# First cross attention of a perceiver block: the softmax's probabilities turned by VectorE and DMA in place of TensorE

## The chip, the cores and the metric

The kernel runs as one program on one NeuronCore of a Trainium2 chip. The metric is the time on the device in microseconds (us); of several executions the median is taken. One further execution was recorded by the hardware profiler. All durations of single instructions come from that one.

The engines are TensorE (PE; its weight loads are shown apart as PEld), VectorE (DVE), ScalarE (ACT), GpSimd (POOL) and SyncE (SP, which here only issues DMAs).

## The reference, cut to what matters

A block of six residual layers works on `x` (32 batches of 64 tokens, 256 features) beside a context `ctx` (32 batches of 256 rows, 256 features). All is float32. The change is in the first layer, a cross attention whose keys and values are the context's rows and the tokens themselves:

```python
def _L0_xattn_ref(image_embeds, latents, ..., Wq, Wkv, Wo):   # ctx, layernorm(x)
    x = layer_norm(image_embeds, ln1_g, ln1_b)      # 32 x 256 x 256
    l = layer_norm(latents, ln2_g, ln2_b)           # 32 x 64 x 256
    q = l @ Wq                                      # 16 heads of 64
    kv_in = jnp.concatenate([x, l], axis=1)         # 320 keys
    k, v = jnp.split(kv_in @ Wkv, 2, axis=-1)
    w = jnp.einsum('bhqd,bhkd->bhqk', q * scale, k * scale)
    w = jax.nn.softmax(w, axis=-1)
    out = jnp.einsum('bhqk,bhkd->bhqd', w, v)
    return out.transpose(0, 2, 1, 3).reshape(B, S_lat, INNER) @ Wo
```

The other layers are a linear attention, a gated feed-forward, a second cross attention, a recurrent gate layer and a mixture of eight experts.

## The kernel before, in words

**An order planned on the host.** Nearly every instruction is first recorded with a length in us, a `rank` (when it should come) and the buffers that it needs, in an object `pl` (class `Plan`). `Plan.run` (line 299) then plays all five engines against these lengths and emits the instructions one after the other: of those that can start first, the one of lowest rank. The order of each engine is thus fixed before the kernel runs, from the model's lengths (`PlanEngine.length`, line 474) and not from what happens on the chip. Copies out of PSUM may go to ACT or to DVE (`pl.copy`, `pl.either`), whichever the model finds earlier. A DMA costs its issuing engine 0.06 us in this model. Because one helper line emits everything, the profile gives line L375 for nearly all instructions; they are told apart by their tiles.

**Buffers.** One large SBUF tile, the arena, holds everything but small vectors; each kind of tile (`ar.put`, from line 649) has one or more fixed places, taken in turn. PSUM is eight banks of 512 floats per partition, all of one kind (`bank`).

**The first layer** goes through 32 batches b, two to a 128-row tile of tokens (16 tiles), four to a group (8 groups), in these steps:

- `l0_context` (777): loads two batches of context into `cx` (2 places) and normalises them.
- `l0_queries` (805), once in four batches: normalises the tokens (`la`, and `ls`, its two halves swapped by two DMAs), multiplies by Wq (PSUM `pq`) and then, head by head, by Wk (PSUM `pqk`), so that scores can be taken directly against the context. The result is one tile `qk` for the group, with one place: 16 heads stand in 8 pairs j, a pair's two heads and 64 tokens being 128 columns.
- `l0_keys` (857): transposes the batch's context into `cT` and puts the tokens' columns beside it, once on each side: 64 + 256 + 64 columns.
- `l0_scores` (872): for each of the 8 pairs, two passes over 128 features give `sc`, 128 rows (2 heads x 64 tokens) by 320 keys, in one PSUM bank. DVE takes the negated maximum (`nmax`), ACT takes the exponential with its sum (`sm`) into `pr`, DVE inverts `sm` and multiplies the 320 columns by it: one small and one larger DVE instruction for each pair. The pairs come as jj = 0 (j = 0, 2, 4, 6) and jj = 1; the keys' order is tokens-context for jj = 0 and context-tokens for jj = 1, so that in `pr` the two token parts stand side by side.
- `l0_applied` (902): the probabilities must stand with the keys on the partitions. Per batch TensorE transposes 16 blocks of 128 x 128 (`pTp`, four to a bank) and 4 more for the token keys (`plp`); five copies bring them to SBUF (`pT00` to `pT11`, `pl`). Then `pu` = context^T times probabilities: per half of the features and per jj two matmuls of 512 columns over 128 keys, and one over the 64 token keys; for these last the two jj use the upper and the lower half of the array's rows. Copies go to `uT`.
- `l0_projected` (939), once in two batches: `uT` times Wv (PSUM `po`), times Wo (`pw`), added to `x`.

A float32 matmul appears as two MATMUL instructions, a transpose as one. The model's lengths for PE are written beside the code, e.g. `with pl.together(T4)` with T4 = 0.46 us for four transposes.

What sets the order around the change is the ranks: scores of batch b have b - 0.7 to b, `l0_applied` has b, the projection 2t + 1.6. `pl.run(12.0)` lets the plan look 12 ranks ahead, so that the second stage's first work fills in at the end of this layer. Later tiles of the second stage take over places of the arena when the first layer's last tiles leave them.

Of the kernel before, what the change touches and what calls it, by code (L numbers as in the profile page):

```python
# [438 lines left out]
class PlanEngine:  # L439
# [33 lines left out]
    @staticmethod  # L473
    def length(engine, name, args, kw):

        if "dma" in name:
            return 0.06 if "indirect" not in name else 1.55 if "compute_op" in kw else 1.25
# [21 lines left out]
def kernel(ctx: ExitStack, tc: tile.TileContext, d: dict, out: bass.AP):  # L499
# [96 lines left out]
    def experts_constants():  # L596
# [10 lines left out]
        nc.gpsimd.memset(rst[:, :, 0:1], 0.0)  # L607
        c["ones"] = ones = e1.tile([P, P], F32, tag="ones", name="ones")
        nc.gpsimd.memset(ones, 1.0)

# [15 lines left out]
    ec = experts_constants()  # L626
    irow, slot, sp1, i8, rk, rst, ones, tok0, before, thr = (
        ec[n] for n in ("irow", "slot", "sp1", "i8", "rk", "rst", "ones", "tok0", "before", "thr")
    )
# [3 lines left out]
    with ExitStack() as sa:  # L633
        ARENA = 44928
        arena = sa.enter_context(tc.tile_pool(name="arena", bufs=1)).tile([P, ARENA], F32, tag="arena", name="arena")
# [19 lines left out]
        ar.put(1, "cx", 1024, 14336, 15360)  # L655
        ar.put(1, "cT", 768, 16384, 17152)
        ar.put(0, "gbcol", 256, 17920, 18176)
        ar.put(1, "qk", 8192, 17920)
        ar.put(1, "uT", 4096, 26112)
        ar.put(1, "pr", 640, *range(30208, 35328, 640))  # L660
        for n, tag in enumerate(("pT00", "pT01", "pT10", "pT11", "pl")):
            ar.put(1, tag, 512, 35328 + 1024 * n, 35840 + 1024 * n)
        ar.put(1, "oT", 1024, 40448)

        for tag, size, *at in (
# [15 lines left out]
            ("g_tmp", 128, 41472), ("g_tmp2", 128, 41600), ("g_h", 128, 41728),  # L681
            ("a_wq", 512, 41856), ("a_wkv", 1024, 42368), ("rows_a", 1024, 43392),
        ):
# [121 lines left out]
        def l0_queries(g):  # L805
# [37 lines left out]
            pl.rank = G * g - 0.9  # L843
            qk = ar.tile([P, KD, G, 8, 2, S], F32, tag="qk", name=f"qk{g}")
            for n in range(8):
                j = 2 * (n % 4) + n // 4
                pqk = [bank([P, KD, G * S], f"pqk{g}_{j}_{i}") for i in range(2)]
                with pl.together(1.0):
                    for kd in range(KD):
                        for i in range(2):  # L850
                            h_ = slice(64 * i, 64 * i + 64)
                            mm(pqk[i][:, kd], wkT[h_, j, kd * P : (kd + 1) * P], q[h_, j, :], start=True, stop=True)
                for i in range(2):
                    pl.copy(qk[:, :, :, j, i, :], pqk[i].rearrange("p k (b s) -> p k b s", b=G))
            return la, ls, lt, qk

        def l0_keys(b, lt, cx):

            pl.rank, pl.lane = b - 1.2, "k"
            b2, b4 = b % 2, b % G  # L860
            cT = ar.tile([P, KD, SK + S], F32, tag="cT", name=f"cT{b}")
# [5 lines left out]
            for c0 in (0, SK):  # L867
                pl.gpsimd.tensor_copy(cT[:, :, c0 : c0 + S], lt[:, :, b4 * S : (b4 + 1) * S])
            pl.copy(cT[:, :, S:SK], pst)
            return cT  # L870

        def l0_scores(b, cT, qk):

            pl.lane = "s"
            prs = [ar.tile([P, 2 * SK], F32, tag="pr", name=f"pr{b}_{i}", bufs=8) for i in range(4)]
            for jj in range(2):
                k0 = 0 if jj else S
                for jp in range(4):  # L880
                    j = 2 * jp + jj
                    pl.rank = b - 0.7 + 0.1 * (4 * jj + jp)
                    sc = bank([P, SK], f"sc{b}_{j}")
                    with pl.together(1.1):
                        for kd in range(KD):
                            mm(
                                sc,
                                qk[:, kd, b % G, j].rearrange("p i s -> p (i s)"),
                                cT[:, kd, k0 : k0 + SK],
                                start=(kd == 0),  # L890
                                stop=(kd == KD - 1),
                            )
                    nmax = sp.tile([P, 1], F32, tag="nmax", name=f"nmax{b}_{j}")
                    pl.vector.tensor_reduce(nmax, sc, AX.X, ALU.max, negate=True)
                    sm = sp.tile([P, 1], F32, tag="sm", name=f"sm{b}_{j}")
                    pr = prs[jp][:, jj * SK : (jj + 1) * SK]
                    pl.scalar.activation(pr, sc, AF.Exp, bias=nmax, accum_out=sm)
                    pl.vector.reciprocal(sm, sm)
                    pl.vector.tensor_scalar(pr, pr, sm, None, ALU.mult)
            return prs  # L900

        def l0_applied(b, prs, cx, la, ls, uT):

            pl.rank, pl.lane = float(b), "a"
            bp, b2 = b // 2 % 2, b % 2
            pT = [[], []]
            for jj in range(2):
                for n in range(2):
                    pT_ = ar.tile([P, 4, P], F32, tag=f"pT{jj}{n}", name=f"pT{b}_{jj}_{n}")
                    pTp = bank([P, 4, P], f"pTp{b}_{jj}_{n}")  # L910
                    with pl.together(T4):
                        for jp in range(4):
                            c0 = jj * SK + n * P + (S if jj else 0)
                            tr(pTp[:, jp, :], prs[jp][:, c0 : c0 + P], ident)
                    pl.copy(pT_, pTp)
                    pT[jj].append(pT_)
            pl_ = ar.tile([P, 4, P], F32, tag="pl", name=f"pl{b}")
            pl_ps = bank([P, 4, P], f"plp{b}")
            with pl.together(T4):
                for jp in range(4):  # L920
                    tr(pl_ps[:, jp, :], prs[jp][:, S2 : S2 + P], ident)
            pl.copy(pl_, pl_ps)

            lk = [la, ls] if b2 == 0 else [ls, la]
            for kd in range(KD):
                f_ = slice(kd * P, (kd + 1) * P)
                pus = [bank([P, 4, P], f"pu{b}_{kd}_{jj}") for jj in range(2)]
                for jj in range(2):
                    with pl.together(1.75):
                        for n in range(2):  # L930
                            mm(pus[jj], cx[:, 2 * b2 + n, f_], pT[jj][n], start=(n == 0), stop=False)
                with pl.together(0.9):
                    for jj in range(2):
                        h_ = slice(64 * jj, 64 * jj + 64)
                        mm(pus[jj], lk[jj][h_, bp, f_], pl_[h_], start=False, stop=True)
                for jj in range(2):
                    pl.copy(uT[:, kd, 4 * jj : 4 * jj + 4, :, b2, :], pus[jj].rearrange("p j (i s) -> p j i s", i=2))

# [26 lines left out]
        for t in range(NTILE):  # L965
            cx = l0_context(t)
            uT = None
            for b in (2 * t, 2 * t + 1):
                if b % G == 0:
                    la, ls, lt, qk = l0_queries(b // G)  # L970
                cT = l0_keys(b, lt, cx)
                prs = l0_scores(b, cT, qk)
                if uT is None:

                    uT = ar.tile([P, KD, 8, 2, 2, S], F32, tag="uT", name=f"uT{t}")
                l0_applied(b, prs, cx, la, ls, uT)
            l0_projected(t, uT)
# [541 lines left out]
        def cells(part, gate, cap, first=None):  # L1519
# [15 lines left out]
            pl.scalar.copy(gT, gT_ps)  # L1535
            v.tensor_tensor_scan(rank, ones, sel, 0.0, ALU.mult, ALU.add)
            cnt = rank[:, P - 1 : P]
# [277 lines left out]
        v.tensor_reduce(ext, thr_, AX.X, ALU.add)  # L1815
        v.tensor_tensor_scan(cum, ones[:, 0:E], ext, 0.0, ALU.mult, ALU.add)
        v.tensor_tensor(ext, cum, ext, ALU.subtract)
# [105 lines left out]
```

## Time and profile before

| | us |
|---|---|
| median of 3 runs | 1720.64 |
| lowest, highest | 1719.38, 1720.93 |
| the profiled execution's own time | 1723.92 |
| its span, first to last instruction | 1722.2 |
| TensorE busy | 1653.6 (96%) |
| VectorE busy | 1034.1 (60%) |
| ScalarE busy | 696.6 (40%) |
| GpSimd busy | 316.1 (18%) |
| mean granted TensorE clock | 0.988 |

The first score matmul starts at 31.2 us and the last first-layer projection ends near 920 us: the first layer is a little over half of the span. In a busy share the ends of matmuls are modelled, and two matmuls can overlap; how fast PE goes is read from the distance between the starts of successive matmuls. The group rows give a mean duration of one instruction, which for a matmul is longer than that distance. A releaser behind an arrow is what ended an engine's idle time.

### The profile page before, as it was taken

What the parts mean: (1) busy time and instruction counts of PE and PEld (TensorE: products, weight loads), DVE (VectorE), ACT (ScalarE), POOL (GpSimd) and SP (SyncE); (2) the same over time, 40 slices, a digit from 0 to 9 for tenths busy, and PEclk for the clock granted to TensorE, in tenths of its full rate; (3) what the DMA queues carried; (4) which work ended last, traced back from release to release, by engine and by line L of the source; (5) the groups of instructions that cost most, each with busy time, mean ns of one, the idle gap of its engine ahead of it and who ended that gap; (6) DMA issues with size and microseconds to landing.
All of it is one profiled execution on the core that took longest, in us unless ns stands there. A gap on an engine that the chain in (4) does not pass through costs nothing. (4 is left out here: it accounts for less than half of the span.)

```text
span 1722.2 us, 26712 instructions
## 1 busy us (share of the span) xinstructions
PE 1653.6 (96%) x9866; PEld 1174.4 (68%) x9866; DVE 1034.1 (60%) x3430; ACT 696.6 (40%) x1830; POOL 316.1 (18%) x413
## 2 busy tenths in 40 slices
PE   7999999999999999999998799999999998999996
PEld 6666666766666766666565576777777776788885
DVE  7546464555554644645444578878888787853131
ACT  4334343443433433434331145545455455623232
POOL 5102120121111210211001211212202121133233
PEclk9999999999999999999999899999999999999998
DMA  6000000000000000001001000000100112255292
GB/s 206 13 7 25 7 25 13 6 20 13 19 7 13 13 13 6 19 7 59 25 1 59 13 1 26 26 19 20 38 13 26 58 44 73 68 162 166 38 295 57
DMA packets 50548, 74.09 MB, mean 43 GB/s; under 512 B 5231, under 2 KB 40880, under 8 KB 50416
## 3 DMA queue, kind: packets, MB, share of 16 engines
q1 hardware_dynamic: 44896, 64.42, 11.9%
q0 software_dynamic: 5520, 7.94, 2.2%
q8 instruction: 79, 1.29, 0.3%
q14 instruction: 53, 0.43, 0.1%
HBM read 63.63 MB, written 7.47 MB: 41 GB/s over the span
## 5 line engine op out<-in xcount | busy, mean ns | idle before, releaser
L375 PE MATMUL pu<-arena 128*128 128x512 f32 (+1 forms) x768 | 299.1, 613 | 0.0
L375 PE MATMUL sc<-arena 128*128 128x320 f32 x1024 | 298.6, 437 | 0.0
L375 PEld LDWEIGHTS sc<-arena 128*128 128x128 f32 x1024 | 187.5, 190 | 88.2 <-issue 21.1
L375 PEld LDWEIGHTS pu<-arena 128*128 128x128 f32 (+1 forms) x768 | 111.4, 188 | 164.6 <-issue 164.4
L375 ACT ACTIVATE arena<-sc,nmax 128x320 f32<-128x320 f32 x256 | 135.4, 529 | 182.3 <-DVE nmax L375 182.2
L375 POOL TENSOR_TENSOR arena<-arena 128x256 f32<-128x256 f32 (+3 forms) x104 | 137.5, 1325 | 255.1 <-DVE arena L375 214.9
L375 DVE TENSOR_REDUCE nmax<-sc 128x1 f32<-128x320 f32 x256 | 124.3, 489 | 90.6 <-PE sc L375 84.7
L375 DVE COPY arena<-pu 128x512 f32<-128x512 f32 x64 | 44.3, 692 | 215.6 <-PE pu L375 215.4
L375 ACT ACTIVATE arena<-arena,xnm 128x256 f32<-128x256 f32 x256 | 127.2, 499 | 58.6 <-DVE xnm L375 58.0
L375 ACT COPY arena<-pu 128x512 f32<-128x512 f32 x64 | 37.5, 586 | 242.9 <-PE pu L375 242.9
L375 DVE TENSOR_SCALAR arena<-arena,sm 128x320 f32<-128x320 f32 x256 | 117.5, 459 | 9.0
L375 DVE CUSTOM_DVE_ANT_0 arena<-xsc,arena 128x256 f32<-128x256 f32 x256 | 100.9, 420 | 9.3 <-ACT arena L375 3.8
L375 POOL TENSOR_TENSOR r_c<-ve_c,mhalf 128x4 f32<-128x4 f32 x16 | 16.3, 1019 | 310.0 <-DVE sm L375 258.7
L375 PEld LDWEIGHTS pTp<-ident,arena 128*128 128x128 f32 x512 | 59.4, 141 | 14.3 <-ACT arena L375 2.3
L375 PE MATMUL pTp<-ident,arena 128*128 128x128 f32 x512 | 67.6, 274 | 0.9 <-DVE arena L375 0.8
L375 PE MATMUL xpTp<-ident,arena 128*128 128x128 f32 x512 | 63.7, 274 | 2.2 <-ACT arena L375 1.8
L375 PE MATMUL xav<-arena 128*128 128x256 f32 x256 | 63.0, 391 | 0.4 <-DVE arena L375 0.4
L375 PEld LDWEIGHTS xpTp<-ident,arena 128*128 128x128 f32 x512 | 57.3, 141 | 8.8 <-DVE arena L375 2.9
L375 PE MATMUL xak<-arena 128*128 128x512 f32 x128 | 62.9, 617 | 0.1
L375 PE MATMUL mepha<-arena 128*128 128x256 f32 x256 | 60.0, 385 | 1.4 <-ACT arena L375 1.4
L375 PE MATMUL pq<-arena 128*128 128x256 f32 x256 | 60.1, 380 | 0.7 <-ACT arena L375 0.7
L375 ACT COPY arena<-xpTp 128x512 f32<-128x512 f32 x80 | 44.5, 585 | 39.0 <-PE xpTp L375 39.0
(407 smaller groups left out, 2916.3 us busy)
## 6 DMA issues: line engine op xcount, KB each, us to landing
arena<-in_m_w SPq DMA_DIRECT2D x26, 1024.0 KB
arena<-in_ctx SPq DMA_DIRECT2D x32, 256.0 KB
arena<-in_ctxT SPq DMA_DIRECT2D x16, 512.0 KB
x<-in_x SPq DMA_DIRECT2D x16, 128.0 KB
arena<-in_l0x_wkv SPq DMA_DIRECT2D x2, 1024.0 KB
arena<-arena SPq DMA_DIRECT2D x16, 128.0 KB
out<-x SPq DMA_DIRECT2D x16, 128.0 KB
xd<-arena SPq DMA_DIRECT2D x16, 128.0 KB
```

The costliest lines, as they stand in the source:

```text
L375: r = getattr(real, name)(*[get(a) for a in args], **{k: get(a) for k, a in kw.items()})
```

## The change

In the first layer:

- The 20 TensorE transposes per batch, their five PSUM banks and their five copies go. In their place DVE transposes 32 x 32 blocks: for each jj, two instructions of 512 columns and one of 256 write from `pr` into a new tile `bT` (one place), in which each group of 32 partitions still holds the wrong rows of blocks. Then 16 DMAs per batch, issued by SP, move blocks between the four groups of partitions into `pT` (2 places): DMA (k, a) takes partitions 32a to 32a+31, column group k, five runs of 128 floats per partition, to partitions 32k to 32k+31. That is 160 runs of 512 bytes, 80 KB; 16 of them are 1.25 MB per batch.
- `pr` now holds one jj of a batch (four pairs by 320 columns, 3 places). The normalisation is done for four pairs at once: one reciprocal of 4 values and one tensor_tensor multiply of 1280 columns with a broadcast operand, in place of four reciprocals and four tensor_scalar multiplies of 320.
- The keys' order is context-tokens for all pairs, so `cT` loses its third part and GpSimd one of its two copies.
- `pu`'s matmuls read `pT` through a pattern of runs of 32 columns, where they read 512 consecutive columns. Their number is the same.
- `qk` is eight tiles, one for each pair, with eight places, where it was one tile; the scores take them pair by pair.
- Ranks: scores at b - 1.6 + ..., the normalisation and transposes 0.3 below the last score of their jj. The model's cost of issuing a plain DMA goes from 0.06 to 0.4 us for all DMAs of the kernel; its length for the pair of token-key matmuls goes from 0.9 to 1.04.

In the mixture layer the constant tile of ones is dropped: two cumulative sums are written with add and max in place of multiply and add, with the same sizes. The places in the arena are laid out anew; it grows by 128 columns.

```diff
         if "dma" in name:
-            return 0.06 if "indirect" not in name else ...
+            return 0.4 if "indirect" not in name else ...
...
-        ar.put(1, "cT", 768, 16384, 17152)
+        ar.put(1, "cT", 640, 16384, 17024)
-        ar.put(1, "qk", 8192, 17920)
+        ar.put(1, "qk", 1024, *range(17664, 25856, 1024))
-        ar.put(1, "pr", 640, *range(30208, 35328, 640))
-        for n, tag in enumerate(("pT00", "pT01", "pT10", "pT11", "pl")):
-            ar.put(1, tag, 512, 35328 + 1024 * n, 35840 + 1024 * n)
+        ar.put(1, "pr", 1280, 29952, 31232, 32512)
+        ar.put(1, "bT", 2560, 33792)
+        ar.put(1, "pT", 2560, 36352, 38912)
...
         def l0_scores(b, cT, qk):
             pl.lane = "s"
-            prs = [ar.tile([P, 2 * SK], F32, tag="pr", ...) for i in range(4)]
+            B_ = 32
+            bT = ar.tile([P, 5, 4, 4, B_], F32, tag="bT", name=f"bT{b}")
             for jj in range(2):
-                k0 = 0 if jj else S
+                pr = ar.tile([P, 4, SK], F32, tag="pr", name=f"pr{b}_{jj}")
+                sm = sp.tile([P, 4], F32, tag="sm", name=f"sm{b}_{jj}")
                 for jp in range(4):
                     j = 2 * jp + jj
-                    pl.rank = b - 0.7 + 0.1 * (4 * jj + jp)
+                    pl.rank = b - 1.6 + 0.1 * (4 * jj + jp)
...
-                    pl.scalar.activation(pr, sc, AF.Exp, bias=nmax, accum_out=sm)
-                    pl.vector.reciprocal(sm, sm)
-                    pl.vector.tensor_scalar(pr, pr, sm, None, ALU.mult)
-            return prs
+                    pl.scalar.activation(pr[:, jp, :], sc, AF.Exp, bias=nmax, accum_out=sm[:, jp : jp + 1])
+                pl.rank -= 0.3
+                pl.vector.reciprocal(sm, sm)
+                pl.vector.tensor_tensor(pr, pr, sm.unsqueeze(2).to_broadcast([P, 4, SK]), ALU.mult)
+                for n in range(2):
+                    pl.vector.transpose(
+                        bT[:, 2 * n + jj].rearrange("p k j c -> p j k c"),
+                        pr[:, :, n * P : (n + 1) * P].rearrange("p j (k c) -> p j k c", c=B_),
+                    )
+                pl.vector.transpose(
+                    bT[:, 4, 2 * jj : 2 * jj + 2].rearrange("p k j c -> p j k c"),
+                    pr[:, :, S2:SK].rearrange("p j (k c) -> p j k c", c=B_),
+                )
+            pT = ar.tile([P, 5, 4, 4, B_], F32, tag="pT", name=f"pT{b}")
+            for k in range(4):
+                for a in range(4):
+                    pl.sync.dma_start(
+                        out=pT[B_ * k : B_ * k + B_, :, a].rearrange("p m j c -> p m (j c)"),
+                        in_=bT[B_ * a : B_ * a + B_, :, k].rearrange("p m j c -> p m (j c)"),
+                    )
+            return pT
...
         def l0_applied(b, pT, cx, la, ls, uT):
-            pT = [[], []]
-            for jj in range(2):
-                for n in range(2):
-                    pT_ = ar.tile([P, 4, P], F32, tag=f"pT{jj}{n}", name=f"pT{b}_{jj}_{n}")
-                    pTp = bank([P, 4, P], f"pTp{b}_{jj}_{n}")
-                    with pl.together(T4):
-                        for jp in range(4):
-                            c0 = jj * SK + n * P + (S if jj else 0)
-                            tr(pTp[:, jp, :], prs[jp][:, c0 : c0 + P], ident)
-                    pl.copy(pT_, pTp)
-                    pT[jj].append(pT_)
-            pl_ = ar.tile([P, 4, P], F32, tag="pl", name=f"pl{b}")
-            pl_ps = bank([P, 4, P], f"plp{b}")
-            with pl.together(T4):
-                for jp in range(4):
-                    tr(pl_ps[:, jp, :], prs[jp][:, S2 : S2 + P], ident)
-            pl.copy(pl_, pl_ps)
...
-                            mm(pus[jj], cx[:, 2 * b2 + n, f_], pT[jj][n], start=(n == 0), stop=False)
-                with pl.together(0.9):
+                            rhs = pT[:, 2 * n + jj].rearrange("p a j c -> p j a c")
+                            mm(pus[jj], cx[:, 2 * b2 + n, f_], rhs, start=(n == 0), stop=False)
+                with pl.together(1.04):
...
-            v.tensor_tensor_scan(rank, ones, sel, 0.0, ALU.mult, ALU.add)
+            v.tensor_tensor_scan(rank, sel, sel, 0.0, ALU.add, ALU.max)
```

More of the change, by code (lines that the diff above doesn't have):

```diff
@@ L476, in length @@
         if "dma" in name:
-            return 0.06 if "indirect" not in name else 1.55 if "compute_op" in kw else 1.25
+            return 0.4 if "indirect" not in name else 1.55 if "compute_op" in kw else 1.25
         o = args[0] if args else kw["out"]
@@ L607, in experts_constants @@
         nc.gpsimd.memset(rst[:, :, 0:1], 0.0)
-        c["ones"] = ones = e1.tile([P, P], F32, tag="ones", name="ones")
-        nc.gpsimd.memset(ones, 1.0)
         c["tok0"] = tok0 = e1.tile([P, 1], F32, tag="tok0", name="tok0")
@@ L626 @@
     ec = experts_constants()
-    irow, slot, sp1, i8, rk, rst, ones, tok0, before, thr = (
-        ec[n] for n in ("irow", "slot", "sp1", "i8", "rk", "rst", "ones", "tok0", "before", "thr")
+    irow, slot, sp1, i8, rk, rst, tok0, before, thr = (
+        ec[n] for n in ("irow", "slot", "sp1", "i8", "rk", "rst", "tok0", "before", "thr")
     )
@@ L633 @@
     with ExitStack() as sa:
-        ARENA = 44928
+        ARENA = 45056
         arena = sa.enter_context(tc.tile_pool(name="arena", bufs=1)).tile([P, ARENA], F32, tag="arena", name="arena")
@@ L655 @@
         ar.put(1, "cx", 1024, 14336, 15360)
-        ar.put(1, "cT", 768, 16384, 17152)
-        ar.put(0, "gbcol", 256, 17920, 18176)
-        ar.put(1, "qk", 8192, 17920)
-        ar.put(1, "uT", 4096, 26112)
-        ar.put(1, "pr", 640, *range(30208, 35328, 640))
-        for n, tag in enumerate(("pT00", "pT01", "pT10", "pT11", "pl")):
-            ar.put(1, tag, 512, 35328 + 1024 * n, 35840 + 1024 * n)
-        ar.put(1, "oT", 1024, 40448)
+        ar.put(1, "cT", 640, 16384, 17024)
+        ar.put(0, "gbcol", 256, 17664, 17920)
+        ar.put(1, "qk", 1024, *range(17664, 25856, 1024))
+        ar.put(1, "uT", 4096, 25856)
+        ar.put(1, "pr", 1280, 29952, 31232, 32512)
+        ar.put(1, "bT", 2560, 33792)
+        ar.put(1, "pT", 2560, 36352, 38912)
+        ar.put(1, "oT", 1024, 41472)
         for tag, size, *at in (
@@ L681 @@
             ("g_tmp", 128, 41472), ("g_tmp2", 128, 41600), ("g_h", 128, 41728),
-            ("a_wq", 512, 41856), ("a_wkv", 1024, 42368), ("rows_a", 1024, 43392),
+            ("a_wq", 512, 42496), ("a_wkv", 1024, 43008), ("rows_a", 1024, 44032),
         ):
@@ L843, in l0_queries @@
             pl.rank = G * g - 0.9
-            qk = ar.tile([P, KD, G, 8, 2, S], F32, tag="qk", name=f"qk{g}")
+            qk = [None] * 8
             for n in range(8):
                 j = 2 * (n % 4) + n // 4
+                qk[j] = ar.tile([P, KD, G, 2, S], F32, tag="qk", name=f"qk{g}_{j}")
                 pqk = [bank([P, KD, G * S], f"pqk{g}_{j}_{i}") for i in range(2)]
@@ L853, in l0_queries @@
                 for i in range(2):
-                    pl.copy(qk[:, :, :, j, i, :], pqk[i].rearrange("p k (b s) -> p k b s", b=G))
+                    pl.copy(qk[j][:, :, :, i, :], pqk[i].rearrange("p k (b s) -> p k b s", b=G))
             return la, ls, lt, qk
@@ L860, in l0_keys @@
             b2, b4 = b % 2, b % G
-            cT = ar.tile([P, KD, SK + S], F32, tag="cT", name=f"cT{b}")
+            cT = ar.tile([P, KD, SK], F32, tag="cT", name=f"cT{b}")
             pst = bank([P, KD, S2], f"tr_c{b}")
@@ L866, in l0_keys @@
                         tr(pst[:, kd, i * P : (i + 1) * P], cx[:, 2 * b2 + i, kd * P : (kd + 1) * P], ident)
-            for c0 in (0, SK):
-                pl.gpsimd.tensor_copy(cT[:, :, c0 : c0 + S], lt[:, :, b4 * S : (b4 + 1) * S])
-            pl.copy(cT[:, :, S:SK], pst)
+            pl.gpsimd.tensor_copy(cT[:, :, S2:SK], lt[:, :, b4 * S : (b4 + 1) * S])
+            pl.copy(cT[:, :, 0:S2], pst)
             return cT
@@ L876, in l0_scores @@
             pl.lane = "s"
-            prs = [ar.tile([P, 2 * SK], F32, tag="pr", name=f"pr{b}_{i}", bufs=8) for i in range(4)]
+            B_ = 32
+            bT = ar.tile([P, 5, 4, 4, B_], F32, tag="bT", name=f"bT{b}")
             for jj in range(2):
-                k0 = 0 if jj else S
+                pr = ar.tile([P, 4, SK], F32, tag="pr", name=f"pr{b}_{jj}")
+                sm = sp.tile([P, 4], F32, tag="sm", name=f"sm{b}_{jj}")
                 for jp in range(4):
                     j = 2 * jp + jj
-                    pl.rank = b - 0.7 + 0.1 * (4 * jj + jp)
+                    pl.rank = b - 1.6 + 0.1 * (4 * jj + jp)
                     sc = bank([P, SK], f"sc{b}_{j}")
@@ L887, in l0_scores @@
                                 sc,
-                                qk[:, kd, b % G, j].rearrange("p i s -> p (i s)"),
-                                cT[:, kd, k0 : k0 + SK],
+                                qk[j][:, kd, b % G].rearrange("p i s -> p (i s)"),
+                                cT[:, kd, :],
                                 start=(kd == 0),
@@ L894, in l0_scores @@
                     pl.vector.tensor_reduce(nmax, sc, AX.X, ALU.max, negate=True)
-                    sm = sp.tile([P, 1], F32, tag="sm", name=f"sm{b}_{j}")
-                    pr = prs[jp][:, jj * SK : (jj + 1) * SK]
-                    pl.scalar.activation(pr, sc, AF.Exp, bias=nmax, accum_out=sm)
-                    pl.vector.reciprocal(sm, sm)
-                    pl.vector.tensor_scalar(pr, pr, sm, None, ALU.mult)
-            return prs
-        def l0_applied(b, prs, cx, la, ls, uT):
+                    pl.scalar.activation(pr[:, jp, :], sc, AF.Exp, bias=nmax, accum_out=sm[:, jp : jp + 1])
@@ L904, in l0_applied @@
+            pT = ar.tile([P, 5, 4, 4, B_], F32, tag="pT", name=f"pT{b}")
[6 more added lines that the diff above has]
+            return pT
+        def l0_applied(b, pT, cx, la, ls, uT):
             pl.rank, pl.lane = float(b), "a"
@@ L926, in l0_applied @@
                 f_ = slice(kd * P, (kd + 1) * P)
-                pus = [bank([P, 4, P], f"pu{b}_{kd}_{jj}") for jj in range(2)]
+                pus = [bank([P, 4, 4, 32], f"pu{b}_{kd}_{jj}") for jj in range(2)]
                 for jj in range(2):
@@ L930, in l0_applied @@
                         for n in range(2):
-                            mm(pus[jj], cx[:, 2 * b2 + n, f_], pT[jj][n], start=(n == 0), stop=False)
-                with pl.together(0.9):
+                            rhs = pT[:, 2 * n + jj].rearrange("p a j c -> p j a c")
+                            mm(pus[jj], cx[:, 2 * b2 + n, f_], rhs, start=(n == 0), stop=False)
+                with pl.together(1.04):
                     for jj in range(2):
                         h_ = slice(64 * jj, 64 * jj + 64)
-                        mm(pus[jj], lk[jj][h_, bp, f_], pl_[h_], start=False, stop=True)
+                        rhs = pT[h_, 4].rearrange("p a j c -> p j a c")
+                        mm(pus[jj], lk[jj][h_, bp, f_], rhs, start=False, stop=True)
                 for jj in range(2):
-                    pl.copy(uT[:, kd, 4 * jj : 4 * jj + 4, :, b2, :], pus[jj].rearrange("p j (i s) -> p j i s", i=2))
+                    pl.copy(
+                        uT[:, kd, 4 * jj : 4 * jj + 4, :, b2, :],
+                        pus[jj].rearrange("p j (i a) c -> p j i (a c)", i=2),
+                    )
         def l0_projected(t, uT):
@@ L971 @@
                 cT = l0_keys(b, lt, cx)
-                prs = l0_scores(b, cT, qk)
+                pT = l0_scores(b, cT, qk)
                 if uT is None:
                     uT = ar.tile([P, KD, 8, 2, 2, S], F32, tag="uT", name=f"uT{t}")
-                l0_applied(b, prs, cx, la, ls, uT)
+                l0_applied(b, pT, cx, la, ls, uT)
             l0_projected(t, uT)
@@ L1815 @@
         v.tensor_reduce(ext, thr_, AX.X, ALU.add)
-        v.tensor_tensor_scan(cum, ones[:, 0:E], ext, 0.0, ALU.mult, ALU.add)
+        v.tensor_tensor_scan(cum, ext, ext, 0.0, ALU.add, ALU.max)
         v.tensor_tensor(ext, cum, ext, ALU.subtract)
```

## The prediction

> **What bounds the kernel now.** I read the page's busy shares first, then the slices, then the windows over the first layer, then the timeline of TensorE inside it.
>
> ```profile
> PE 1653.6 (96%) x9866; PEld 1174.4 (68%) x9866; DVE 1034.1 (60%) x3430; ACT 696.6 (40%) x1830; POOL 316.1 (18%) x413
> ...
> PE   7999999999999999999998799999999998999996
> ...
> PEclk9999999999999999999999899999999999999998
> ```
>
> TensorE is busy in every slice. In the first layer (slices 2 to 21) it has no gap, and the clock is full. SP's timeline shows a load of context every 111.67 us (starts at 165.52, 277.19, 388.86, 500.53, 612.21): one group of four batches, 27.92 us a batch. The windows of such groups:
>
> ```profile
> 277.19:388.86 111.67, 111.67 (x582) 73.67 (x582) 61.80 (x167) 43.90 (x108) 17.05 (x17) 1.00 0.06 15
> 388.86:500.53 111.67, 111.67 (x582) 73.67 (x582) 60.56 (x167) 43.80 (x108) 16.97 (x17) 1.00 0.05 13
> ```
>
> The columns are length, busy PE, PEld, DVE, ACT, POOL, then clock, DMA share, GB/s. PE fills the window to the last tenth, DVE has 60.6 of 111.67 (15.1 us a batch), DMA a share of 0.05. A full busy share alone doesn't show that PE streams without a pause, so I read distances between starts:
>
> ```profile
> 508.50 1.04 PE L375 MATMUL pTp<-ident,arena 128*128 128x128 f32 x8
> 509.37 1.89 PE L375 MATMUL pq<-arena 128*128 128x256 f32 x8
> 511.10 1.04 PE L375 MATMUL pTp<-ident,arena 128*128 128x128 f32 x8
> 511.97 0.60 PE L375 MATMUL plp<-ident,arena 128*128 128x128 f32 x4
> 512.41 5.29 PE L375 MATMUL pu<-arena 128*128 128x512 f32 x13
> ```
>
> Eight transposes take 509.37 - 508.50 = 0.87 us, 109 ns each; four plp 0.44. Eight pq of 256 columns take 1.73, 216 ns: twice the columns, twice the time. The stream is dense. What leaves it shortens the layer one for one, as long as its operands come in time.
>
> **Removed from PE.** 20 transposes a batch, 640 in all, at 109 ns: 2.18 us a batch, **69.8 us**. The rows of groups give 273 ns as the mean of one, because a matmul's duration holds its pipeline; 640 x 273 would be 175 us and is wrong here, where the next one starts after 109. (The Trainium skill, "TensorE: Matmul & The Clock Gate", Part 4: PE-mode transpose, gives about 275 ns for one in a kernel's context: the duration rows agree with it. By that rule the sum would be 176 us; by the distances it is 70, and the measurement decides.)
>
> New length of a batch: 27.92 - 2.18 = 25.74 us. The other matmuls keep their number and size.
>
> **VectorE**, a batch:
>
> ```profile
> L375 DVE TENSOR_SCALAR arena<-arena,sm 128x320 f32<-128x320 f32 x256 | 117.5, 459 | 9.0
> L375 DVE RECIPROCAL sm<-sm 128x1 f32<-128x1 f32 x256 | 40.0, 156 | 24.7 <-ACT arena L375 23.0
> L375 DVE COPY arena<-pTp 128x512 f32<-128x512 f32 x60 | 40.9, 686 | 13.4 <-PE pTp L375 13.4
> L375 DVE COPY arena<-plp 128x512 f32<-128x512 f32 x22 | 15.2, 691 | 4.5 <-PE plp L375 4.5
> ...
> L375 DVE TENSOR_TENSOR x<-x,arena x16: 410/420/949, 939.2 to 1382.9; 128x256 f32<-128x256 f32 x16
> ```
>
> Off: six of eight reciprocals, 0.94; eight multiplies, 8 x 0.459 = 3.67; DVE's share of the copies, (40.9 + 15.2)/32 = 1.75. On: two multiplies of 1280 columns. A tensor_tensor of 256 has a median of 420 ns (last line: min/median/max); the copies give 686 for 512, so one column costs 1.04 ns and the start 0.155 us: 1.49 each, 2.97 for two. Transposes of 32 x 32 blocks are in no row. If they run like the copies, four of 512 and two of 256 cost 4 x 0.686 + 2 x 0.42 = 3.58. Below, half of it is possible; above, the slowest row per element is the reciprocal (253 ns for 16 values, 156 for one: 6.5 ns each), 2560 x 6.5 = 16.6. I take 3.58, the plain streaming rate, as for every copy here. Sum: 15.1 - 0.94 - 3.67 - 1.75 + 2.97 + 3.58 = 15.3 us of 25.74: 59%, covered. At 16.6 it would be 28.3, more than a batch takes now. ACT only loses copies; GpSimd loses one copy a batch. The cumulative sums keep their sizes: nothing.
>
> **The way round by DMA.** SP's timeline has a row for 16 small DMAs, a packet size comes from the windows around single loads:
>
> ```profile
> 914.69 7.52 SPq L375 DMA_DIRECT2D arena<-in_x_wo  x16
> ...
> 581.00:584.00 3.00, 3.00 (x22) 2.22 (x20) 2.86 (x10) 2.04 (x4) 1.44 (x2) 1.00 0.41 87
> 612.00:616.00 4.00, 4.00 (x16) 2.35 (x16) 1.56 (x3) 1.20 (x3) 0.00 (x0) 1.00 0.22 66
> ```
>
> Sixteen issues take 7.52 us, 0.47 each, so SP is busy for 7.5 of 25.74 us. Context rows (1 KB): share 0.22 x 16 engines x 4 us = 14.1 engine-us for 264 KB, 55 ns each. The swapped halves, SBUF to SBUF (2 KB runs): 0.41 x 16 x 3 = 19.7 for 261 KB, 154 ns each. A run of 512 bytes lies between a quarter of the last, 38, and all of it, 154; I take 55, the row nearest in size. A batch has 16 x 160 = 2560 runs: 2560 x 55/16 = 8.8 us on 16 engines (6.1 to 24.6). With about 2 us for the last to land (an estimate: the 768 KB of `f_wd`, issued at 922.3, had landed when DVE went on at 927.1) the phase takes 11 us, at most 27.
>
> The cover: ranks put the scores of b+1 (b - 0.6 to b + 0.1) ahead of `l0_applied` of b. Between the last score of b and `pu` of b, PE thus has `pu` of b-1 (9.3 us, from 877.19 to 886.47) and eight scores of b+1 (16 x 2 x 0.27 = 8.6): 17.9 us, and up to 7.8 of projections and queries. The chain is nmax 0.49, exponential 0.73, reciprocal 0.16, multiply 1.49, transposes 1.8, hops 0.4: 5.1, and then 11: 16. It fits, by 2 to 10 us. If that cover fails, PE waits the difference in each batch: 1 us costs 32 us in all.
>
> Two more waits. `bT` has one place: the first DVE transpose of b+1 must wait until all 16 DMAs of b have read it, and behind it in DVE's queue stand `nmax` and the copies of `pu`, for which PSUM and then PE would wait. The loop is 3.6 + 11 = 15 us against 25.74: free. On SP the DMAs stand in one queue with the context loads, which now sit at its head for up to 76 us (4 issues from 500.53); the plan puts them in the order of its own start times, and 7.5 us of issuing is little against 25.74. A place of `cx` comes free after one `pu` and is wanted again about two batches later.
>
> (The Trainium skill, "DMA: Bandwidth & Descriptors", Anatomy of one DMA, gives 2.0 us + bytes/436e3 for a GpSimd-issued DMA, and its Rules say that below 64 KB one pays mostly overhead. Sixteen of 80 KB one after the other would take 35 us a batch by it, and the change would lose; the row of `x_wo`, 16 issued in 7.52 us, says that they overlap.)
>
> **The other matmul edits.** `pu` reads runs of 32 columns. No strided stream is in the trace; every PE row goes by its column count alone, so I take nothing. The end above: the token-key pairs take 1.06 us (four MATMULs, two at a time) where 0.86 would be dense, 24% more; on the other `pu` (64 x 0.43 a group) that is 6.6 us a group, 53 in all. `qk` in eight tiles lets copies start earlier; PE waits nowhere for it now: nothing, at best the 3 us a group by which 111.67 exceeds the dense sum of matmuls, 24 in all.
>
> **Ends.** At the start the first `pT` comes 11 us later, but scores of batch 1 and the next group's queries (15 us) lie ready: +2. At the layer's end `pu` of batch 31 comes late, while second-stage loads wait for the last `pw` (weights landed at 927.1, DVE idle 6.4 us, PE 4): +4, up to 10.
>
> **Sum.** 69.8 - 6 = 64 us. Against the profiled execution's own 1723.92: 1660; the median of the runs shown is 3.28 lower, so **1656**.
>
> **Rivals.**
> 1. Partial: PE waits 0.5 to 1.6 us a batch, for late DMAs, for DVE's blocks of 3.3 us ahead of a `nmax`, or by the strided reading. 16 to 53 us are given back: 1672 to 1709, middle 1690. For it: a slack of only 2 us is certain, and the order is fixed on the host. Against: 10 us are likely, and DVE is at 59%.
> 2. Slower, the loop over `bT`: transposes 3.6, then 16 DMAs, then the next transposes. If a run costs 154 ns, the phase is 24.6 + 2 = 26.6 and the loop 30.2 us with no way around it: 32 x (30.2 - 27.92) = +73, so 1794. It decides from a phase of 27.92 - 3.6 = 24.3 us, 139 ns a run; it eats the gain from 22.1, 126 ns. For it: the only SBUF-to-SBUF row. Against: that row's runs are four times as long.
> 3. The cover is so thin that gain and wait cancel: 1720.
>
> **Chances.** Forecast 0.66, partial 0.17, slower 0.12, nothing 0.05. The measurement tells about 0.2% (3.4 us) from no change. Faster 0.84, same 0.04, slower 0.12. Range: down by the 24 us that eight `qk` tiles could give, to 1632; up through most of the partial case, 1705. Below it I leave 0.02, above it 0.16.
>
> **What would show it.** Right: groups 103 us apart in SP's context loads, PE full there at clock 1.00, DVE near 60%, 16 issues in 7 to 8 us, block transposes near 0.69. Wrong: waits of PE's loads for `pu` on DMA, DVE waits on DMA ahead of transposes, `pu` starts more than 0.43 apart, or a longer dip after the layer. The step most likely to fail is the length of the DMA phase.

## The result, and the profile after

The changed kernel takes **1771.62 us** (median of 4 runs, 1769.79 to 1776.33) against 1720.79 for the kernel before, run beside it on the same chip: a ratio of 1.0301, 95% interval 1.028 to 1.0323. The forecast was 1656, faster, with a range of 1632 to 1705; the kernel is slower.

The page of after, its busy shares, the slices and the granted clock (its profiled span is 1774.2 us, before 1722.2):

```profile
PE 1627.1 (92%) x9226; PEld 1122.6 (63%) x9226; DVE 1046.1 (59%) x3152; ACT 657.8 (37%) x1756; POOL 306.0 (17%) x380
...
PE   8899899898998998899887999999999999999996
...
PEclk9999999999999999999998999999999999999998
```

The 640 transposes are gone (9866 - 9226 instructions), yet PE's busy time fell by 26.5 us only, and the time in which PE is not busy rose from 68.6 to 147.1. The eights are all in the first layer. It ends (last `pw` added to `x`) at 992.0 us, where it ended at 920.3: 71.7 later. The rest of the program is 19.7 shorter (782.2 against 801.9): PE is busy 7.5 us less in it, as 39 more of its matmuls (5135 are left for it, where 5174 were) stand ahead of the first layer's end, and idle 12.2 us less. The two make the 52 us.

Two groups of four batches, from one issue of moves on SP to the same place a group later (length, then busy PE, PEld, DVE, ACT, POOL, then clock, DMA share, GB/s):

```profile
278.38:394.59 116.21, 107.25 (x506) 66.51 (x503) 61.62 (x134) 38.45 (x98) 15.75 (x13) 0.96 0.29 59
394.59:510.68 116.09, 107.13 (x506) 66.44 (x504) 62.41 (x135) 38.45 (x98) 15.75 (x13) 0.96 0.28 57
```

The prediction wanted 103 and a clock of 1.00. PE lacks 9 us of being full, and in what it does it is slower: the clock is 0.96. What it waits for is in the list of waits (engine, tile, releaser: us in all, times, longest):

```profile
PEld pu L375 <- issue: 269.6, 490, 8.3
PE pu L375 <- DMA arena<-arena: 81.0, 19, 7.8
DVE arena L375 <- DMA arena<-arena: 50.5, 17, 5.1
```

`pu` stands still for the moved blocks 19 times, 81.0 us in all. (The first line, weight loads that wait for nothing the profile shows, is probably no cause of its own: 164 us of it stand in the kernel before and 159 in run 3 below, where `pu` waits for a move once. The 110 us above that are about what the pauses and the slow `pu` behind them make.) PE's timeline through the second of those groups shows which batches (start, length, instructions; in brackets the idle time before):

```profile
412.22 9.35 PE L375 MATMUL pu<-arena 128*128 128x512 f32 x24
421.49 2.42 PE L375 MATMUL sc<-arena 128*128 128x320 f32 x8
423.75 1.04 PE L375 MATMUL tr_c<-ident,arena 128*128 128x128 f32 x8
424.62 1.89 PE L375 MATMUL pq<-arena 128*128 128x256 f32 x8
426.35 8.78 PE L375 MATMUL sc<-arena 128*128 128x320 f32 x32
440.77 11.22 PE L375 MATMUL pu<-arena 128*128 128x512 f32 x24 [5.64 <-DMA arena<-arena]
...
475.72 2.42 PE L375 MATMUL sc<-arena 128*128 128x320 f32 x8
477.98 0.60 PE L375 MATMUL tr_c<-ident,arena 128*128 128x128 f32 x4
478.51 7.18 PE L375 MATMUL pqk<-arena 64*128 64x256 f32 x64
485.62 0.66 PE L375 MATMUL tr_c<-ident,arena 128*128 128x128 f32 x4
486.11 6.62 PE L375 MATMUL sc<-arena 128*128 128x320 f32 x24
495.76 11.03 PE L375 MATMUL pu<-arena 128*128 128x512 f32 x24 [3.02 <-DMA arena<-arena]
```

Call the batch of the `pu` at 412.22 b - 1. The eight `sc` instructions at 421.49 are two pairs, the **last two of b** (a pair is four instructions). Behind them come eight pairs of b + 1, and then `pu` of b, which waits. So `pu` of b - 1 is not between the last scores of b and `pu` of b; it runs ahead of both. What PE has there lasts from 423.75 to 435.13, 11.4 us, and chain and moves took 423.75 to 440.77, 17.0. In the second case it is 14.8 us (477.98 to 492.74) against 17.8. Between the two stands a `pu` at 466.45 that doesn't wait: all its scores were done by 435.

A pause costs twice. The 24 matmuls of an undisturbed `pu` take 9.35 us, these 11.22 and 11.03. Three windows behind the first pause:

```profile
440.70:442.70 2.00, 1.93 (x3) 0.93 (x4) 1.92 (x5) 0.00 (x0) 0.00 (x0) 0.50 0.00 0
442.70:444.70 2.00, 2.00 (x4) 0.82 (x3) 1.97 (x3) 0.00 (x0) 0.00 (x0) 0.58 0.00 0
444.70:446.70 2.00, 2.00 (x6) 0.68 (x6) 0.92 (x3) 0.00 (x0) 0.00 (x0) 1.00 0.03 6
```

The granted clock is 0.50, then 0.58, then full. (The Trainium skill, "TensorE: Matmul & The Clock Gate", Part 1: The HAM clock gate, says that the clock falls to one half after an idle window of some 3.4 us and returns after a busy one. The half agrees, and so does the return after nearly 4 us. The length does not: the pause of 3.02 us sufficed, and in these traces one of 2.62 did too.) Per group: the two pauses, 8.7 us, and the four `pu`, 40.65 us from start to next start where the best version below has 37.19: 3.5 slower. Together 12.1, and 116.1 - 12.1 = 104.0, within 0.2 us of the length that the best version has.

### The profile page after: what moved, and what is told of

Same layout as the page of the kernel before. It is cut to its first block, busy times and chain, and to the rows that moved or that the text cites. A ratio compares the mean times of both kernels' runs of the same rounds, so it can differ in the third digit from the quotient of the medians.

```text
span 1774.2 us, 25917 instructions
## 1 busy us (share of the span) xinstructions
PE 1627.1 (92%) x9226; PEld 1122.6 (63%) x9226; DVE 1046.1 (59%) x3152; ACT 657.8 (37%) x1756; POOL 306.0 (17%) x380
## 2 busy tenths in 40 slices
DMA packets 140657, 116.01 MB, mean 65 GB/s; under 512 B 13423, under 2 KB 130992, under 8 KB 140528
## 5 line engine op out<-in xcount | busy, mean ns | idle before, releaser
L375 PE MATMUL pu<-arena 128*128 128x512 f32 (+1 forms) x768 | 333.7, 662 | 81.0 <-DMA arena<-arena 81.0
L375 PEld LDWEIGHTS pu<-arena 128*128 128x128 f32 (+1 forms) x768 | 124.9, 205 | 277.4 <-issue 269.6
L375 PE MATMUL sc<-arena 128*128 128x320 f32 x1024 | 293.1, 438 | 0.3 <-ACT arena L375 0.3
L375 PEld LDWEIGHTS sc<-arena 128*128 128x128 f32 x1024 | 191.5, 191 | 93.8 <-issue 18.6
L375 DVE STREAM_TRANSPOSE arena<-arena 128x512 f32<-128x512 f32 (+1 forms) x192 | 104.3, 594 | 52.1 <-DMA arena<-arena 50.5
L375 ACT COPY arena<-pu 128x512 f32<-128x512 f32 x64 | 37.5, 586 | 240.6 <-PE pu L375 240.6
L375 DVE TENSOR_TENSOR arena<-arena,sm 128x1280 f32<-128x1280 f32 x64 | 95.5, 1492 | 2.2
L375 PEld LDWEIGHTS po<-arena 128*64 128x64 f32 x1024 | 55.3, 137 | 14.5 <-issue 11.3
L375 PE MATMUL po<-arena 128*64 128x128 f32 x1024 | 62.1, 275 | 1.8 <-ACT arena L375 1.8
```

The lines of the kernel that those rows point to most:

```text
L375: r = getattr(real, name)(*[get(a) for a in args], **{k: get(a) for k, a in kw.items()})
```

## The experiments

Each is an edit of the changed kernel, timed against the kernel before on the same chip. The chips differ from run to run (the kernel before takes 1720.48 to 1724.36 us on them), so runs on different chips are best compared by their ratios.

**1. What the moves are worth: all left out.** The 16 DMAs go, and `pu` reads `bT`, which gets `pT`'s place as its second.

```diff
-        ar.put(1, "bT", 2560, 33792)
+        ar.put(1, "bT", 2560, 33792, 36352)
...
-            pT = ar.tile([P, 5, 4, 4, B_], ...); 16 x pl.sync.dma_start(...)
-            return pT
+            return bT
```

> The 16 DMAs of each batch are left out and pu reads bT itself, which gets two places; so blocks stay in the wrong group of partitions, and the rest (block transposes, order of keys, pairs of queries, strided reads) is kept. Theory A: without the way round the matmul gain is whole, 69.8 us off, and no pause: 1640 to 1665. Rival B (strided reads or VectorE's new work are the loss): stays above 1740. Rival C (the DMA phase): like A, 1640 to 1665; this run tells A and C from B alone.

1678.31 us, ratio 0.9751 (0.9735 to 0.9768). No wait of PE for a DMA is left, a group takes 104.2 us and the first layer ends at 859. The loss is in the moves, not in VectorE's new work or the strided reading. The 1678 itself is not the price of the rest: the values are other ones, so tokens can go to other experts, and PE runs 9280 instructions in place of 9226. All 54 more are in tiles of the mixture layer (`mephm`, `mepym` and three small ones) that the changed kernel's trace doesn't have.

**2. The plan told the DMAs' true length.** SP's timeline of the changed kernel has 16 moves issued in 10.32 us, 0.645 each; the plan reckons with 0.4.

```profile
958.34 10.32 SPq L375 DMA_DIRECT2D arena<-arena  x16
```

```diff
-            return 0.4 if "indirect" not in name else ...
+            return 0.65 if "indirect" not in name else ...
```

> The changed kernel with one number altered: the plan counts 0.65 us for the issue of a plain DMA in place of 0.4. No instruction is added or taken away; only the host's order can change. Theory A (the order): TensorE stands 3 to 8 us before pu in every second batch, because the plan reckons 16 x 0.4 + 1.9 = 8.3 us from the last block transpose to pT and the chip takes 12 (16 issues of 0.64 and 2.1 to land); the clock that drops after such a pause comes on top. Told the truth the plan fills part of the pause with scores: between 1700 and 1755. Rival B (strided reads make pu slow, and the pauses only show it): the same as the changed kernel, 1771 within 5. Rival C (the DMA phase is too long for any order, with one bT and three pr): the same, 1771 within 10, with pauses moved to another place.

1692.04 us, ratio 0.9821 (0.9798 to 0.9845). PE's waits for moves fall from 81.0 us (19) to 14.2 (6), and a group takes 105.4. The work is the same; only its order is another. Nearly all that is left stands at the layer's two ends: 7.84 us at 90.52, 4.58 at 829.84; the other four waits are under 0.5 us each.

**3. The order alone.** `pu` gets a rank above the last scores of the next batch (b + 0.1); the plan's length stays 0.4.

```diff
-            pl.rank, pl.lane = float(b), "a"
+            pl.rank, pl.lane = float(b) + 0.15, "a"
```

> The changed kernel with only the rank of l0_applied raised from b to b + 0.15; the plan still counts 0.4 us for an issue. The last two scores of b+1 (ranks b and b + 0.1) then come ahead of pu of b in every batch, and pu of b-1 ahead of nothing of b: between the last score of b and pu of b stand pu of b-1 (9.3 us) and eight scores (8.6), which is the cover that the prediction counted on, against a chain of 5.1 + 12.4. Theory A (the order fixed on the host lets the cover shrink to eight scores): nearly all pauses go though the plan's number stays wrong, 1660 to 1695. Rival C (no order helps, the loop over one bT and three pr binds): 1740 or more. Rival D (what helped in the run that was told 0.65 was another spacing of SyncE's queue and not TensorE's order): 1740 or more too.

**1666.51 us**, ratio 0.9664 (0.9648 to 0.968). One number, 0.15, is worth 105 us between the medians, 110 between the ratios. Two groups of this kernel in the same columns as above, and three lines of PE's timeline:

```profile
245.47:350.43 104.96, 104.90 (x502) 64.61 (x501) 60.28 (x130) 40.07 (x102) 16.97 (x13) 1.00 0.31 66
350.43:455.37 104.94, 104.88 (x502) 64.59 (x501) 60.27 (x130) 40.08 (x102) 16.95 (x13) 1.00 0.32 66
```

```profile
382.81 8.78 PE L375 MATMUL sc<-arena 128*128 128x320 f32 x32
391.42 9.35 PE L375 MATMUL pu<-arena 128*128 128x512 f32 x24
...
857.29 10.98 PE L375 MATMUL pu<-arena 128*128 128x512 f32 x24 [3.11 <-DMA arena<-arena]
```

PE fills the group at full clock. Now all eight pairs of the next batch, with no rest, stand ahead of `pu`, and that batch's own `pu` comes at 419.18: 27.8 us behind its last score, where the chain and the moves need 17 to 18. One wait of PE for a move is left, the 3.11 us at 857.29, at the layer's end, and two of DVE, 1.7 us together, although `bT` still has one place and 16 moves still take 10.33 us to issue.

**4. Order and length together.** Both edits.

> Both: 0.65 us for an issue in the plan and l0_applied at b + 0.15. Theory A: no pause in the middle of the layer, groups of four batches at 103 to 105 us; the start and the end keep some. 1660 to 1685. Rivals C and D: not below the 1692 of the run that was told 0.65 alone.

**1660.53 us**, ratio 0.9625 (0.9609 to 0.9641): the fastest of all. A group:

```profile
402.63:506.42 103.79, 103.26 (x500) 65.26 (x500) 60.23 (x131) 39.97 (x101) 15.68 (x13) 1.00 0.32 64
```

PE's busy time is 1589.6 us, 64.0 below that of before; the time without work is 69.2, 0.6 above it. One pause remains, 5.52 us at 850.66, at the end of the layer.

**5. Longer runs.** With the column group as `bT`'s and `pT`'s outermost index a move has 32 runs of 2560 bytes in place of 160 of 512.

```diff
-            bT = ar.tile([P, 5, 4, 4, B_], ...)     # pT the same
+            bT = ar.tile([P, 4, 5, 4, B_], ...)
...
-                        in_=bT[B_ * a : B_ * a + B_, :, k].rearrange("p m j c -> p m (j c)"),
+                        in_=bT[B_ * a : B_ * a + B_, k].rearrange("p m j c -> p (m j c)"),
```

> The same 16 DMAs with the same bytes, but bT and pT have the group of 32 ahead of the five blocks, so that a partition's 2560 bytes are one run in place of five runs of 512: 32 runs a DMA in place of 160. The plan's numbers are untouched, so its order is the same. If the issue of 0.64 us is long because of the 160 runs, it falls toward 0.47 (the row of 16 small DMAs of the kernel before): phase 16 x 0.47 + 2.1 = 9.6 in place of 12.3, every pause 2.7 us shorter, some 19 of them gone or halved. Theory A: 1700 to 1740. Rival B: 1771. If the number of runs plays no part in the issue: 1765 to 1775.

1764.22 us, ratio 1.0249 (1.0231 to 1.0266); PE still waits 74.8 us (19 times). The packets of the whole program fall from 140657 to 75121, but 16 issues take 10.01 us against 10.32. What a move costs SP hangs on the move and hardly on its runs: a fifth of them saves 3%.

**6. Two queues.** Every second move is issued by ScalarE.

```diff
-                    pl.sync.dma_start(
+                    (pl.sync if a % 2 else pl.scalar).dma_start(
```

> Every second of the 16 DMAs is issued by ScalarE in place of SyncE; sizes and number are the same. Theory A: issue is what fills the phase (16 x 0.64 = 10.3 of 12.3 us), the DMA engines are at 57% in it; two issuers make it 8 x 0.64 + 2.1 = 7.2, less than the 8.3 that the old plan counted: nearly no pause, 1660 to 1710. If the 16 DMA engines are the limit instead, the phase stays near 12 and the time above 1755. ScalarE loses 5 us of 26 a batch to issuing and can hold up exponentials: that is the reason for the upper half of the range.

1695.6 us, ratio 0.9859 (0.9842 to 0.9877). The list of waits of this kernel:

```profile
ACT arena L375 <- DMA arena<-arena: 157.0, 23, 8.2
PE pu L375 <- DMA arena<-arena: 26.4, 17, 4.5
```

The phase is shorter: eight issues take each engine 5.7 to 7.2 us, where sixteen took SP 10.3. PE's wait falls to a third. But a move waits on ScalarE for the blocks, and behind it in ScalarE's queue stand exponentials and copies out of PSUM: a group takes 108 us. A move's landing goes from 2.1 to 3.1 us. (The Trainium skill, "DMA: Bandwidth & Descriptors", Issuing engines are not separate DMA queues, says that several issuing engines share the same 16 DMA engines and save only the time of issuing. That agrees in direction: issuing is what gets shorter, though not by half, and the landing grows.)

**7. Two queues on top of 4.**

> As the last, and every second of the 16 DMAs issued by ScalarE. Theory A: the phase of 7 to 8 us also fits where few matmuls lie ready, at the start and the end of the layer: 1650 to 1680, a few us below the last one. Against it: ScalarE waits on VectorE's transposes with exponentials queued behind, as the 157 us of ScalarE's waits for DMA in the first run with two queues show; then 1680 to 1700.

1692.18 us, ratio 0.9804 (0.9787 to 0.982), 32 us more than without. ScalarE waits 147.5 us for moves, and since PE waits for a move only once in run 4 (5.52 us), hardly anything can be gained for it.

**8. TensorE's transposes put back**, the rest of the change kept (eight `qk` tiles, the joint multiply, the new ranks, one order of keys). The token part needs 8 plain matmuls with the identity where the kernel before had 4 transposes.

```diff
+                            tr(pTp[:, jp, :], prs[jj][:, jp, n * P : (n + 1) * P], ident)
+                            # token part, for each jj:
+                            mm(pTp[64 * jj : 64 * jj + 64, jp, :], prs[jj][:, jp, S2:SK], ident, ...)
```

> The change without its new way of transposing: the 20 transposes a batch are back on TensorE (the four of the token keys as eight plain matmuls with the identity, to 64 partitions each, about 0.5 us a batch more than transposes), and the rest stays (pairs of queries, one normalisation for four pairs, order of keys, ranks, 0.4 in the plan). If those other parts are worth nothing, as predicted: 1720 + 32 x 0.5 = 1736, between 1720 and 1750. If they cost (ranks, order): above 1755. If they bring something: below 1715.

1756.18 us, ratio 1.0182 (1.0165 to 1.0199). The first layer ends 37.5 us later than before. One group takes 117.2 us against 111.7, 5.6 more. Summing the distances between starts over it: transposes take 11.74 against 8.89 us, `pu` 0.4 more, a pause for VectorE ahead of `sc` 1.03, and the last 1.3 is spread in tenths over `sc`, `pqk` and others. Eight times the 2.85 us of the transposes, 23 us, is the price of this experiment's own token part; nearly 15 of the 37.5 are left. Two more runs tried whether the plan had a hand in these 15.

**9. The same with the plan's DMA length back at 0.06.**

> The changed kernel with TensorE's transposes put back (as in the run of that name) and the plan's length for issuing a DMA put back from 0.4 to 0.06 us. Without the sixteen moves a batch hardly any DMA is left in the first layer, so the plan's length for them should not matter there. Theory A (the 16 us that the run with TensorE's transposes lost beyond its sixteen extra matmul halves a batch come from the split qk tiles and the scores' later normalisation, not from the DMA length): within 5 us of 1756. Theory B (the raised length holds up other work of the plan, the second stage's loads above all): 1740 or less.

1765.76 us, ratio 1.0264 (1.0246 to 1.0281): 10 us worse than run 8, 14 by the ratios, which neither theory had. The raised length isn't what costs run 8 its 15 us; that it moves the time at all shows once more that the plan's lengths are part of the kernel. The pause of 1.04 us stays.

**10. The same with rank b + 0.15.**

> The changed kernel with TensorE's transposes put back, and the rank of l0_applied raised from b to b + 0.15, so that the last two pairs of scores of the next batch come ahead of it. Here no DMA phase has to be covered; what stands between the last scores and the first transposes is one chain of 3 us (maximum, exponential, reciprocal, multiply). Theory A (the rank matters only because of the DMA phase): no change beyond 5 us from 1756. Theory B (the rank ends the 1.03 us wait for VectorE that a group shows, and the wait at the start): 1740 to 1750.

1758.57 us, ratio 1.0237 (1.0207 to 1.0267): theory A, no gain over run 8 (2 us worse, 9 by the ratios). The pause for VectorE goes, and one of 0.89 us for GpSimd comes. So the rank that is worth over 100 us beside the moves is worth nothing where no moves have to be covered.

## Why the prediction was wrong, point by point

- **The failed step is the cover**: "ranks put the scores of b+1 (b - 0.6 to b + 0.1) ahead of `l0_applied` of b", and from it "PE thus has `pu` of b-1 ... and eight scores of b+1: 17.9 us". The sentence refutes itself: b + 0.1 is above b. The last score's rank is higher than that of `pu`, the one before it has the same, so both may come behind it, and did, as soon as the plan believed the moves to have landed. With them the anchor slips: `pu` of b - 1 runs ahead of the last scores of b and covers nothing. The 17.9 us became 11.4 and 14.8. Run 3 shows it: with the rank alone changed, the waits fall from 81.0 us (19) to 3.1 (1).
- **The plan's own lengths decide when a rank counts.** 16 x 0.4 us and its landing end sooner in the plan than on the chip; told 0.65 (run 2), the plan finds most of the right order without a new rank.
- **The phase: nearly right, for other reasons.** 17.0 and 17.8 us from last score to `pu` were forecast as 16. An issue takes 0.645 us, not the 0.47 of `x_wo`'s row: 0.175 x 16 = 2.8 us a batch more, and issuing, not the engines, fills the phase. The landing is 2.1, as estimated. The engines, which I let set the phase at 8.8 us, do not: over the phase from 428.60 to 440.80 their share is 0.57, 0.57 x 16 x 12.20/2560 = 43 ns a run against 55. A phase of 12 us would have fitted in the cover that I believed in, if only just (17.0 and 17.8 against 17.9).
- **"1 us costs 32 us in all"** was too low a price: each of the 19 pauses, of 1.90 to 7.84 us, also slowed the `pu` behind it, which took 10.81 to 11.89 us in place of 9.35, 1.5 to 2.5 more.
- **Removed from PE: nearly right.** Run 4 has 64.0 us less busy time on PE and practically the same rest; that the forecast sum was 64 too is partly luck, as it was made of 69.8 us less work and 6 us more waiting. A group lost 7.9 us of the 8.7 forecast, 103.8 against 103; the layer ends 47.0 us earlier, and the rest of the program is 16.4 shorter. The 273 ns of the group rows would have been wrong by more than 100 us.
- **VectorE: right.** The rows that were bounded from other rows, in the groups of after (x count | busy us, mean ns | idle before):

```profile
L375 DVE TENSOR_TENSOR arena<-arena,sm 128x1280 f32<-128x1280 f32 x64 | 95.5, 1492 | 2.2
L375 DVE STREAM_TRANSPOSE arena<-arena 128x512 f32<-128x512 f32 x128 | 83.5, 690 | 52.1 <-DMA arena<-arena 50.5
L375 DVE STREAM_TRANSPOSE arena<-arena 128x256 f32<-128x256 f32 x64 | 25.7, 402 | 0.0
```

They take 1492, 690 and 402 ns, where 1.49, 0.686 and 0.42 us were taken. DVE is busy for 62 of 116 us, 15.5 a batch (15.3).
- **The strided reading: nothing**, right. An undisturbed `pu` takes 9.35 us for its 24 matmuls, before and after.
- **Rival 2, the loop over `bT`,** gave 1794, near the measured time, and is not what happened. DVE does wait 50.5 us for moves to have read `bT`, but in run 3, with the same single place, it waits 1.7 us in all and PE is full. Rival 1 named the mark (PE's waits for moves, an order fixed on the host) but not that the order itself takes the cover away, and its 53 us at most are half of what the pauses took with their slow clock.
- **The eight `qk` tiles** were put at nothing. Run 8 is some 15 us slower than before for all that it keeps of the change; how much of that the tiles cost is open. With the moves the plan orders the pairs otherwise, so it can't be carried over to runs 3 and 4.

What stays open: why an issue of these moves takes 0.645 us and one of `x_wo`'s loads 0.47 (run 5 all but excludes the number of runs; in the changed kernel the 16 loads of `x_wo` themselves take 4.33 us for six and 5.87 for ten, so 0.47 is no fixed price, unless they wait for something there); and whether a second place for `bT`, or an earlier first batch, would end the pauses at the layer's ends. Neither was tried with the moves in place.

## What to carry to other kernels

Where the order of the work is fixed ahead of the run, a latency is covered only by what is *emitted* between producer and consumer; write that order down instruction by instruction from the ranks, ties and the last ones above all, before counting its microseconds. A model's length for a new kind of step must be right before the step is judged: 0.4 in place of 0.645 us, with a rank 0.15 too low, turned the fastest of these kernels (run 4) into one slower than before. Price a pause of TensorE of 2.6 us or more at more than its length.

## What the runs showed of the hardware that had not been expected

- A pause of 3.02 us, and one of 5.64, brought the granted clock to 0.50 at first and to full after 3 to 4 us; the `pu` behind it took 11.03 and 11.22 us in place of 9.35. Over the changed kernel and runs 2 to 7, all 40 pauses of 2.62 us or more ahead of an unbroken `pu` had such a slow one behind them (10.80 us or more), and none of up to 1.88 had (9.42). Between lie seven that don't agree: slow after 1.90, 2.28, 2.29 and 2.47, not after 2.12, 2.23 and 2.58.
- Issuing an 80 KB move between partitions takes SP 0.63 to 0.65 us, with 160 runs of 512 bytes as with 32 of 2560.
- VectorE transposes 32 x 32 blocks of float32 at the rate of a copy: 690 ns for 128 x 512, where a copy of that size took 686.
